# Two pairs of stages merged into one interleaved program, and norms on GpSimd cut in halves

## The chip, the cores and the metric

One core of one Trainium2 chip runs the whole kernel. The metric is the device time of that core in microseconds, as the median of three runs. TensorE is called PE, VectorE DVE, ScalarE ACT, GpSimd POOL, and SP is the engine that issues most transfers.

## The reference

Four batches (B) of 512 tokens with 128 features pass through two layers. Cut to what matters here:

```python
x = L0_attn_x                                           # first layer
x = x + 0.5 * L0_ffn(layernorm(x))                      # latent causal attention, mixture of 8 experts
x = x + L0_attn(layernorm(x))                           # full attention, 16 heads
x = x + 0.5 * L0_ffn(layernorm(x))
x = x + 0.5 * L1_ffn(layernorm(x))                      # second layer: heads of chosen tokens
x = x + L1_attn(layernorm(x))                           # four depths of additive attention and MLP
x = x + 0.5 * L1_ffn(layernorm(x))                      # heads of chosen tokens again
```

`L1_ffn` lets each of 8 heads choose 64 of the 512 tokens by a gate, and attends among these:

```python
logits = sigmoid(einsum('bth,eh->bte', X, Wr))
topk_vals, topk_I = top_k(logits.transpose(0, 2, 1), k)            # k = 64
Q, K, V = split(einsum('beki,eij->bekj', Xg, Wqkv), 3)             # Xg: the chosen tokens
Q, K = rope(Q, topk_I), rope(K, topk_I)
A = softmax(where(topk_I[..., :, None] >= topk_I[..., None, :], Q @ K.T / sqrt(HP), -inf))
out = out.at[idx_flat].add((A @ V * topk_vals[..., None]) @ Wo)
```

A depth of `L1_attn` is, for i in 0 to 3:

```python
h = layernorm(x); q = l2norm(h @ Wq[i] + bq[i]); k = l2norm(h @ Wk[i] + bk[i])
A = l2norm(q @ w_g[i] * SCALE, axis=tokens); G = sum(A * q, axis=tokens)
x = x + ((G * k) @ Wp[i] + bp[i] + q) @ Wf[i] + bf[i]
x = x + gelu(layernorm(x) @ W1[i] + b1[i]) @ W2[i] + b2[i]
```

## The kernel before

`X` and `Y` stay in SBUF as 128 partitions by batch, 4 chunks of tokens and 128 features. All work is written as Python generators that yield between steps. The order in which they are advanced is the order in which instructions are written; each engine then runs a queue of its own, and the queue's order is fixed when the program is built, where an instruction that is ready can be placed ahead of one written earlier. Tiles come from pools. A pool with `bufs=2` has two buffers of each tile, and a pool that is opened after another is closed gets the same memory, so that its first writers wait for the last users.

**First layer.** `first_layer` makes twelve tasks, four batches each of latent, full and latent attention, of 10, 16 and 10 units. `attention()` walks over the units, two half steps to a unit: PE computes scores (L527 for the row maxima, L562 shifted for the exponent), ACT the exponent (L574), POOL the causal masks (L580), PE the products (L605). After each half step `step_background` advances the first generator of `background` and all of `beside`. `prepare` of the next task stands in `background`: layer norm, with `h` (L323) and for latent tasks `Y` (L336) made by POOL in four pieces of 128x128 each, then the transposes and projections. `place` waits for `prepare` and for the end of the task before last, plus `GAP`, then spreads q and k over the partitions. `gates` stands in `beside`: norm (four pieces on POOL, L686), gate logits, expert weights. `Mixture` computes the experts (L472, L473 on POOL) in the half steps that follow.

**Second layer, three stages.** `choice` takes two batches: layer norm into `m_yg` (L182, with the rows of `m_trig` loaded beside), logits (L809), sigmoid with Abs and Exp on ACT (L815, L816), eight rounds of max and replace on DVE (L836, L838), a scan (L846), and the slot numbers `byt` (L854). `chosen_attention` runs the heads of a batch: `pick` (L869, DVE) gathers tokens by matmuls (L880), then projections (L903), rotation (`other`, L917 and L918 on DVE, an add on POOL at L921), scores (L931, L932), Exp (L939), products (L961, L970), and the way back into `X` (L983, L992). Its 15 steps start five apart for neighbouring batches, and the choice of batches 2 and 3 (`others`) starts with it. `additive_attention` runs the four depths of the four batches, with a start five steps apart, 23 steps to a depth: L1142 and L1145, the norms `r` on POOL (L154), L1176, L1188, L1199, L1205, L1209, then the MLP with L1244, Gelu on ACT (L1245), L1250 and L1259. `weights(i)` loads one depth's weights on SP (L1035 to L1045) and folds them by matmuls (L1058 to L1104). Weights 0 are made before the first step, weights i from step 23 (i - 1) + 15 on. At the end a choice of batches 0 and 1 runs beside the last depth.

`in_turn` advances a list of generators, each once in a round. The loop at the end of `tile_macaron` runs `first_layer` and `chosen_attention`, then `additive_attention` and `chosen_attention`, each with pools of its own: `moa` for the heads, `add` and `one` for the depths, `top` for the choices.

Of the kernel before, what the change touches and what calls it, by code (L numbers as in the profile page):

```python
# [8 lines left out]
F32 = mybir.dt.float32  # L9
BF16 = mybir.dt.bfloat16  # L10
AF = mybir.ActivationFunctionType
ALU = mybir.AluOpType
# [28 lines left out]
def tile_macaron(ctx: ExitStack, tc: tile.TileContext, a: dict, out: bass.AP):  # L41
# [31 lines left out]

    def load(name, shape, src, eng=nc.scalar):
        t = const.tile(shape, F32, name=f"sb_{name}")
        eng.dma_start(t, src)
        return t
# [16 lines left out]
    causal = const.tile([P, T], F32, name="causal")  # L94
    paired = const.tile([P, P], BF16, name="paired")
    ones = const.tile([P, T], F32, name="ones")
    zeros = const.tile([4, T], F32, name="zeros")
    before = const.tile([P, NE, NE], F32, name="before")
# [103 lines left out]
    def later(name, shape, *parts):  # L202


        def begin():
            if name not in late:
                late[name] = const.tile(shape, F32, name=f"sb_{name}")
            for where, src in parts:
                dst = late[name] if where is None else late[name][:, where]
                tc.keep_in_program_order(nc.sync.dma_start(dst, src))  # L210

        return begin
# [19 lines left out]
    def first_layer(opened, picked):  # L232
        with (
# [42 lines left out]
            class Task:  # L276
# [24 lines left out]
                def prepare(self):  # L301
# [19 lines left out]
                    for c in range(NC):  # L321
                        at = n - NC + c
                        eng.tensor_scalar(  # L323
                            h[:, c, :], X[:, b, c, :], mv[:, c, 0:1], r[:, at : at + 1], ALU.subtract, ALU.mult
                        )
                    yield
# [7 lines left out]
                    else:  # L334
# [4 lines left out]
                        nc.scalar.activation(hT, transposed(h), AF.Copy, scale=f_cols[:, 0:1])  # L339
                        yield  # L340
# [332 lines left out]
            def gates(task):  # L673
# [11 lines left out]
                for c in range(NC):  # L685
                    nc.gpsimd.tensor_scalar(h[:, c, :], Y[:, b, c, :], r[:, c : c + 1], None, ALU.mult)  # L686
                yield
# [170 lines left out]
    def chosen_attention(top, picked, choosing):  # L858

        with tc.tile_pool(name="moa", bufs=2) as wp:  # L860

            def stream(b):

                yg, byt = picked[b]

                pick = wp.tile([P, NC, NE, KSEL], F32, name="pick")
                for c in range(NC):
                    at = byt[:, c, :].unsqueeze(2).to_broadcast([P, NE, KSEL])
                    nc.vector.tensor_tensor(  # L869
                        pick[:, c], at, slots.unsqueeze(1).to_broadcast([P, NE, KSEL]), ALU.is_equal  # L870
                    )
                yield

                xs = wp.tile([P, NPAIR, YG], F32, name="xs")
                for k in range(2):
                    ps = bank().rearrange("p (i n) -> p i n", i=2)
                    for i in range(2):
                        r = 2 * k + i
                        for c in range(NC):
                            nc.tensor.matmul(  # L880
                                ps[:, i, 0:YG],
                                lhsT=pick[:, c, 2 * r : 2 * r + 2, :].rearrange("p e s -> p (e s)"),
                                rhs=yg[:, c, :],
                                start=(c == 0),
                                stop=(c == NC - 1),
                            )
                    (nc.scalar.copy if k else nc.vector.tensor_copy)(xs[:, 2 * k : 2 * k + 2, :], ps[:, :, 0:YG])
                    yield
                xg = wp.tile([P, T], F32, name="xg")
                nc.scalar.copy(xg, transposed(xs[:, :, 0:P]))  # L890
                own = small.tile([P, NPAIR, NE], F32, name="own")
                nc.gpsimd.tensor_tensor(own, xs[:, :, AT_G : AT_G + NE], mine, op=ALU.mult)
                gate = small.tile([P, NPAIR], F32, name="gate")
                nc.vector.tensor_reduce(gate, own, axis=AX.X, op=ALU.add)
                yield

                qk = wp.tile([P, NPAIR, 2, P], F32, name="qk")
                v = wp.tile([P, NPAIR, P], F32, name="v")
                for r in range(NPAIR):
                    ps = bank()  # L900
                    for i in range(2):
                        e = 2 * r + i
                        nc.tensor.matmul(  # L903
                            ps[i * KSEL : (i + 1) * KSEL, 0 : 3 * P],
                            lhsT=xg[:, e * KSEL : (e + 1) * KSEL],
                            rhs=late["m_wqkv"][:, e, :],
                            start=True,
                            stop=True,
                        )
                    both = ps[:, 0 : 2 * P].rearrange("p (k n) -> p k n", k=2)  # L910
                    halves = both[:, :, 0:NROT].rearrange("p k (h n) -> p k h n", h=2)
                    cos = xs[:, r, P : P + HROT].unsqueeze(1).unsqueeze(1).to_broadcast([P, 2, 2, HROT])
                    sin = xs[:, r, P + HROT : P + NROT].unsqueeze(1).to_broadcast([P, 2, HROT])
                    turned = qk[:, r, :, 0:NROT].rearrange("p k (h n) -> p k h n", h=2)
                    nc.vector.tensor_tensor(turned, halves, cos, ALU.mult)
                    other = wp.tile([P, 2, 2, HROT], F32, name="other")
                    nc.vector.scalar_tensor_tensor(other[:, :, 0, :], halves[:, :, 1, :], -1.0, sin, ALU.mult, ALU.mult)  # L917
                    nc.vector.tensor_tensor(other[:, :, 1, :], halves[:, :, 0, :], sin, ALU.mult)  # L918
                    nc.scalar.copy(qk[:, r, :, NROT:P], both[:, :, NROT:P])
                    nc.scalar.copy(v[:, r, :], ps[:, 2 * P : 3 * P])  # L920
                    nc.gpsimd.tensor_tensor(turned, turned, other, op=ALU.add)  # L921
                    yield
                qT = wp.tile([P, T], F32, name="qT")
                nc.scalar.copy(qT, transposed(qk[:, :, 0, :]))
                kT = wp.tile([P, T], F32, name="kT")
                nc.vector.tensor_copy(kT, transposed(qk[:, :, 1, :]))
                yield
                pscore = bank()
                for r in range(NPAIR):
                    cols = slice(r * P, (r + 1) * P)  # L930
                    nc.tensor.matmul(pscore[:, cols], lhsT=qT[:, cols], rhs=kT[:, cols], start=True, stop=False)  # L931
                    nc.tensor.matmul(pscore[:, cols], lhsT=ident_h, rhs=paired, start=False, stop=True)  # L932
                nm = small.tile([P, NPAIR], F32, name="nmp")
                nc.vector.tensor_reduce(nm, by_chunk(pscore), axis=AX.X, op=ALU.max, negate=True)
                nc.vector.tensor_scalar(nm, nm, P**-0.5, None, ALU.mult)
                total = small.tile([P, NPAIR], F32, name="totalp")
                e_ = wp.tile([P, NPAIR, P], F32, name="e_")
                for r in range(NPAIR):
                    nc.scalar.activation(  # L939
                        e_[:, r, :],  # L940
                        pscore[:, r * P : (r + 1) * P],
                        AF.Exp,
                        bias=nm[:, r : r + 1],
                        scale=P**-0.5,
                        accum_out=total[:, r : r + 1],
                    )
                rt = small.tile([P, NPAIR], F32, name="rtp")
                nc.vector.reciprocal(rt, total)

                back = wp.tile([P, NPAIR, T], F32, name="back")  # L950
                for r in range(NPAIR):
                    nc.vector.tensor_scalar(
                        back[:, r, :], places, xs[:, r, AT_T : AT_T + 1], gate[:, r : r + 1], ALU.is_equal, ALU.mult
                    )
                yield
                eT = wp.tile([P, NPAIR, P], F32, name="eT")
                nc.vector.tensor_copy(eT, by_chunk(transposed(e_)))
                yield
                pav = bank()
                for r in range(NPAIR):  # L960
                    nc.tensor.matmul(  # L961
                        pav[:, r * P : (r + 1) * P], lhsT=v[:, r, :], rhs=eT[:, r, :], start=True, stop=True
                    )
                av = wp.tile([P, T], F32, name="av")
                nc.scalar.copy(av, pav)
                yield
# [397 lines left out]
```

## Time and profile before

| | |
|---|---|
| runs | 1371.43, 1371.81, 1377.16 us; median 1371.81 |
| profiled execution | 1375.36 us, of which 1373.6 us from the first to the last instruction |
| mean granted PE clock | 0.968 |
| PE idle while waiting (by line waited for) | heads' and depths' norms: `h` L1225 8.7 us, `m_yg` L182 6.8 us; masks `e` L580 7.5 us |
| POOL `r` (L154) | 64 of 128x4, mean 1125 ns; 16 of 128x8, mean 1648 ns |
| DVE max and replace (L836, L838) | 32 each, about 0.67 us |
| SP | 4 sets of six weight loads for the depths, 256, 128, 256, 129, 256 and 256 KB |

The page is read from the engine that is busiest down to the places where it isn't: the span is cut in 40 equal slices, and each digit gives a busy share or a clock in tenths. Windows give the same for chosen stretches, in us with the number of instructions in brackets, in the order PE, PE weight loads, DVE, ACT, POOL, then clock, DMA share and GB/s. In timelines and groups, the bracket at the end says how long the engine sat idle before and which instruction released it. A matmul in fp32 leaves two records.

### The profile page before, as it was taken

Reading aid. Unit: us, or ns where it says so; the run is one execution under the profiler, and the core shown is the slowest. Engines: PE = TensorE matmul, PEld = TensorE weight load, DVE = VectorE, ACT = ScalarE, POOL = GpSimd, SP = SyncE. Lnnn points to the kernel's source line nnn. Section 1 sums busy time; section 2 is a strip of 40 time slices with the busy share of each in tenths; the row PEclk is TensorE's granted clock in tenths of the full one; section 3 lists DMA queues with packets and bytes.
Section 4 is the critical chain, followed back from the end, with each engine's and each line's share of the span. In section 5 each row is a group of like instructions: output and inputs, shape, how many; then the busy total and the mean of one; then the engine's idle time right before and its main releaser. Section 6 shows DMA issues by size and latency. Waiting matters only on the chain.

```text
span 1373.6 us, 29346 instructions
## 1 busy us (share of the span) xinstructions
PE 1288.2 (94%) x11050; PEld 699.2 (51%) x11050; DVE 953.5 (69%) x3293; ACT 587.1 (43%) x1180; POOL 563.3 (41%) x823
## 2 busy tenths in 40 slices
PE   5998999999999999999999999989799999997897
PEld 2554444333333333465444443466667767665675
DVE  6886676666657777878767548687466776667773
ACT  1555454454546666655545443222123332323122
POOL 8345655544424202025564655622144443543100
PEclk8999999999999999999999999999969999999799
DMA  3001111020111100000101021000300000000000
GB/s 115 21 24 43 40 33 49 2 80 1 64 44 32 38 2 18 18 3 19 60 22 46 20 71 40 32 0 17 100 20 5 16 1 16 1 1 1 1 9 23
DMA packets 37172, 39.52 MB, mean 29 GB/s; under 512 B 11080, under 2 KB 23880, under 8 KB 37032
## 3 DMA queue, kind: packets, MB, share of 16 engines
q1 hardware_dynamic: 34536, 35.06, 8.1%
q10 hardware_dynamic: 2496, 2.59, 0.6%
q8 instruction: 87, 1.43, 0.4%
q14 instruction: 53, 0.43, 0.1%
HBM read 29.45 MB, written 1.18 MB: 22 GB/s over the span
## 4 chain that ended last, share of the span: by engine, by line
PE 71%; DVE 17%; POOL 9%; issue 2%; ACT 1%; DMA 0%; SPq 0%; DVEq 0%; POOLq 0%; ACTq 0%
PE bank L562 17%; PE sum L605 10%; PE bank L267 10%; PE sum L267 7%; PE bank L527 6%; POOL r L154 4%; PE bank L193 4%; PE bank L880 2%; PE bank L983 2%; DVE st L167 2%; PE bank L1250 2%; PE bank L903 1%; PE bank L1142 1%; PE bank L1244 1%; DVE junk L543 1%
## 5 line engine op out<-in xcount | busy, mean ns | idle before, releaser
L574 ACT ACTIVATE e<-bank 128x512 f32<-128x512 f32 x576 | 313.9, 595 | 276.5 <-PE bank L527 238.0
L527 PE MATMUL bank<-kA,qA 32*128 32x512 f32 (+3 forms) x1536 | 345.6, 524 | 3.8 <-DVE nm L543 1.8
L562 PE MATMUL bank<-qA,kA 32*128 32x512 f32 (+3 forms) x1536 | 331.9, 521 | 0.3 <-DVE nm L543 0.3
L543 DVE CUSTOM_DVE_ANT_0 junk<-bank,causal 128x384 f32<-128x384 f32 (+3 forms) x512 | 251.0, 490 | 88.4 <-PE bank L527 50.2
L547 DVE TENSOR_REDUCE nm<-bank 128x1 f32<-128x512 f32 x256 | 164.9, 686 | 77.4 <-PE bank L527 77.0
L473 POOL TENSOR_TENSOR hid<-v,spread 128x512 f32<-128x512 f32 x128 | 164.1, 1288 | 126.0 <-DVE v L472 101.5
L562 PEld LDWEIGHTS bank<-qA,kA 32*128 32x128 f32 x1536 | 128.5, 184 | 136.6 <-issue 54.8
L605 PE MATMUL sum<-e,vA 128*32 128x256 f32 (+1 forms) x2560 | 183.1, 367 | 7.5 <-POOL e L580 7.5
L580 POOL TENSOR_SCALAR_AFFINE_SELECT e<-e 128x256 f32<-128x256 f32 x256 | 99.7, 409 | 191.3 <-ACT e L574 190.3
L527 PEld LDWEIGHTS bank<-kA,qA 32*128 32x128 f32 x1536 | 146.0, 185 | 23.8 <-DVE nm L543 5.8
L605 PEld LDWEIGHTS sum<-e,vA 128*32 128x32 f32 x2560 | 62.7, 109 | 166.5 <-issue 133.6
L267 PE MATMUL sum<-hid,sb_f_w 128*32 128x512 f32 x1024 | 135.6, 597 | 2.8 <-POOL hid L473 2.7
L267 PE MATMUL bank<-tT,sb_f_w 128*32 128x512 f32 x1024 | 137.1, 602 | 0.0
L472 DVE SCALAR_TENSOR_TENSOR v<-th,bank 128x512 f32<-128x512 f32 x128 | 87.1, 681 | 43.3 <-ACT th L467 28.4
L467 ACT ACTIVATE th<-bank 128x512 f32<-128x512 f32 x128 | 76.4, 598 | 48.5 <-PE bank L267 39.0
L154 POOL TENSOR_TENSOR r<-v,mhalf 128x4 f32<-128x4 f32 (+1 forms) x64 | 71.9, 1125 | 5.1
L1244 PE MATMUL bank<-h2T,w 128*128 128x512 f32 x128 | 69.0, 632 | 0.2 <-ACT h2T L1233 0.2
L1250 PE MATMUL bank<-w,hid 128*128 128x128 f32 x512 | 65.6, 277 | 0.1
L1250 PEld LDWEIGHTS bank<-w,hid 128*128 128x128 f32 x512 | 62.9, 194 | 4.8 <-issue 1.5
L1245 ACT ACTIVATE hid<-bank,sb_l_cols 128x512 f32<-128x512 f32 x64 | 44.0, 689 | 40.1 <-PE bank L1244 39.8
L1142 PE MATMUL bank<-wa,hT 128*128 128x385 f32 x128 | 57.6, 547 | 2.5 <-ACT hT L1135 2.5
L312 POOL TENSOR_SCALAR v<-mv 128x4 f32<-128x4 f32 x12 | 2.8, 231 | 130.8 <-DVE mv L171 130.5
(279 smaller groups left out, 1807.9 us busy)
## 6 DMA issues: line engine op xcount, KB each, us to landing
spread<-away SPq DMA_DIRECT2D x64, 256.0 KB
qA<-mT SPq DMA_DIRECT2D x192, 2.0 KB
qA<-qC SPq DMA_DIRECT2D x11, 256.0 KB
kA<-kC SPq DMA_DIRECT2D x11, 256.0 KB
w<-in_l_w_dram SPq DMA_DIRECT2D x8, 256.0 KB
sb_m_wqkv<-in_m_wqkv_dram SPq DMA_DIRECT2D x4, 384.0 KB
m_yg<-in_m_trig_dram SPq DMA_DIRECT2D x8, 130.0 KB
X<-in_x_dram SPq DMA_DIRECT2D x4, 256.0 KB
```

The source lines that it names most:

```text
L154: last_root[0] = nc.gpsimd.tensor_tensor(r[:, 0:n], src, mhalf[:, 0:n], op=ALU.pow).ins
L267: nc.tensor.matmul(ps[32 * j : 32 * j + 32, :], lhsT=w[:, 32 * j : 32 * j + 32], rhs=rhs, start=start, stop=stop, skip_group_check=True,)
L472: nc.vector.scalar_tensor_tensor(v, th, 1.0, ph, ALU.add, ALU.mult)
L473: nc.gpsimd.tensor_tensor(hid, v, self.spread[e], op=ALU.mult)
L527: nc.tensor.matmul(ps[:, at : at + w], lhsT=t.qA[r0 : r0 + 32, g, c * P : (c + 1) * P], rhs=t.kA[r0 : r0 + 32, g, 0:w], start=True, stop=True,
L543: nc.vector.tensor_tensor_reduce(junk[:, 0:w], src, causal[:, T - w : T], 1.0, NEG, ALU.add, ALU.max, dst)
L547: nc.vector.tensor_reduce(dst, src, axis=AX.X, op=ALU.max)
L562: nc.tensor.matmul(ps[:, at : at + w], lhsT=t.kA[r0 : r0 + 32, g, kc * P : (kc + 1) * P], rhs=t.qA[r0 : r0 + 32, g, q0:T], start=True, sto ...
L574: nc.scalar.activation(es[n][:, j, :], ps, AF.Exp)
L580: nc.gpsimd.affine_select(out=e, in_=e, pattern=[[0, 2], [1, P]], compare_op=ALU.is_ge, fill=0.0, base=0, channel_multiplier=-1,)
L605: nc.tensor.matmul(to[32 * j : 32 * j + 32, q0 + lo - at : q0 + hi - at], lhsT=t.vA[:, kc, 4 * j + g, :], rhs=es[n][:, j, lo:hi], start=fresh,
L1250: nc.tensor.matmul(pm[:, c * P : (c + 1) * P], lhsT=hid[:, f, c * P : (c + 1) * P], rhs=w2[:, f, :], start=(f == 0), stop=(f == 3),)
```

## The change

The two stages of the heads and the stage of the depths become `heads_of_chosen` and `additive_attention`, which return generators, and `second_layer` runs them all in one `in_turn`, in one set of pools. The bodies are the same but for the lines shown. A batch's depths begin when its heads are done and the batch before it is five steps ahead. Weights i begin when batch 0 is 13 steps into depth i - 1 and the last batch has finished depth i - 2. The choice of batches 2 and 3 begins when the heads of batch 1 have begun. Some tiles get one buffer in place of two, since all pools now stand side by side. Tiles that only the first layer uses move to a pool `firsts`, which is closed after it. In the first layer, `prepare` and `gates` yield in the middle of the four pieces of their norms on POOL.

```diff
+    until_first = ExitStack()
+    firsts = until_first.enter_context(tc.tile_pool(name="firsts", bufs=1))
...
@@ prepare
                         eng.tensor_scalar(
                             h[:, c, :], X[:, b, c, :], mv[:, c, 0:1], r[:, at : at + 1], ALU.subtract, ALU.mult
                         )
+                        if c == 1 and self.k:
+                            yield
                     yield
...
                             nc.gpsimd.tensor_scalar(
                                 Y[:, b, c, :], X[:, b, c, :], mv[:, c, 0:1], r[:, c : c + 1], ALU.subtract, ALU.mult
                             )
-                        nc.scalar.activation(hT, transposed(h), AF.Copy, scale=f_cols[:, 0:1])
-                        yield
+                            if c == 1:
+                                nc.scalar.activation(hT, transposed(h), AF.Copy, scale=f_cols[:, 0:1])
+                                yield
@@ gates
                     nc.gpsimd.tensor_scalar(h[:, c, :], Y[:, b, c, :], r[:, c : c + 1], None, ALU.mult)
+                    if c == 1:
+                        yield
                 yield
@@ heads_of_chosen
-                pick = wp.tile([P, NC, NE, KSEL], F32, name="pick")
+            pick = wp.tile([P, NC, NE, KSEL], F32, name="pick", bufs=1)
...
+            qk = wp.tile([P, NPAIR, 2, P], F32, name="qk", bufs=1)
...
+                other = wp.tile([P, 2, 2, HROT], F32, name="other", bufs=1)
...
+            qT = wp.tile([P, T], F32, name="qT", bufs=1)
+            kT = wp.tile([P, T], F32, name="kT", bufs=1)
+            eT = wp.tile([P, NPAIR, P], F32, name="eT", bufs=1)
+            av = wp.tile([P, T], F32, name="av", bufs=1)
@@ additive_attention, weights: wqk, bqk, wpT, wfg, L and bpw with bufs=1
-                for _ in range(3):
+            for _ in range(3 if i else 6):
                     yield
@@ additive_attention, stream
             for i in range(DEPTH):
+                while i not in ready:
+                    yield
...
+    def second_layer(top, picked, choosing):
+        STEPS = 23
+        with (
+            tc.tile_pool(name="moa", bufs=2) as cp,
+            tc.tile_pool(name="add", bufs=2) as wp,
+            tc.tile_pool(name="one", bufs=1) as hp,
+        ):
+            heads = heads_of_chosen(cp)
+            additive, weights, depths = additive_attention(wp, hp)
+            again = {}
+            done = {picked_: [0] * B for picked_ in (0, 1)}
+            deep, through = [0] * B, set()
+            def headed(n, b):
+                now = (picked, again)[n]
+                while b not in now or (b > 0 and done[n][b - 1] < 5):
+                    yield
+                for _ in heads(b, now):
+                    done[n][b] += 1
+                    yield
+                done[n][b] = 99
+            def deepened(b):
+                while done[0][b] < 99 or (b > 0 and deep[b - 1] < STEPS // B):
+                    yield
+                for _ in additive(b):
+                    deep[b] += 1
+                    yield
+                deep[b] += STEPS
+                through.add(b)
+            def prepared(i):
+                while i > 0 and (deep[0] < STEPS * (i - 1) + 13 or depths[B - 1] < i - 1):
+                    yield
+                yield from weights(i)
+            def chosen(now, n):
+                while done[n][1] < 1:
+                    yield
+                yield from choice([2, 3], (lambda b: True) if n == 0 else through.__contains__, top, now)
+            def chosen_again():
+                while min(done[0]) < 99:
+                    yield
+                yield from choice([0, 1], through.__contains__, top, again)
+            in_turn(
+                [(0, choosing)]
+                + [(0, headed(0, b)) for b in range(B)]
+                + [(0, chosen(picked, 0))]
+                + [(0, deepened(b)) for b in range(B)]
+                + [(0, prepared(i)) for i in range(DEPTH)]
+                + [(0, chosen_again())]
+                + [(0, headed(1, b)) for b in range(B)]
+                + [(0, chosen(again, 1))]
             )
...
+        chosen_first = first_layer(opened, {})
+        until_first.close()
+        second_layer(*chosen_first)
```

## Prediction

> **What bounds the kernel now.** I read the page first (busy shares, slices, chain), then the waits of PE, then tables of windows, then timelines at the places where the windows show holes.
>
> ```profile
> PE 1288.2 (94%) x11050; PEld 699.2 (51%) x11050; DVE 953.5 (69%) x3293; ACT 587.1 (43%) x1180; POOL 563.3 (41%) x823
> ...
> PE   5998999999999999999999999989799999997897
> ...
> PEclk8999999999999999999999999999969999999799
> ...
> PE 71%; DVE 17%; POOL 9%; issue 2%; ACT 1%; DMA 0%; SPq 0%; DVEq 0%; POOLq 0%; ACTq 0%
> ```
>
> The reader is to see an engine that works nearly always: 1373.6 - 1288.2 = 85.4 us of the span have no matmul. So the change can give only where PE has holes or a slow clock. Slices 29 (busy) and 30 (clock) and slices 37 and 38 (both) say where, at 34.3 us each: 962 to 1030 us and 1236 to 1305 us. Windows there (columns: engine busy us and count, then the clock):
>
> ```profile
> 990.00:1000.00 10.00, 6.42 (x26) 4.07 (x26) 6.39 (x45) 1.93 (x7) 3.20 (x3) 0.81 0.05 14
> ...
> 1260.00:1270.00 10.00, 5.52 (x44) 4.86 (x44) 9.13 (x22) 1.32 (x3) 1.62 (x3) 0.96 0.01 2
> 1270.00:1280.00 10.00, 4.32 (x16) 3.01 (x16) 7.67 (x23) 1.12 (x3) 1.27 (x2) 0.50 0.00 0
> ```
>
> The first hole is a wall between stages, as the timeline shows:
>
> ```profile
> 974.30 3.84 PE L983 MATMUL bank<-xp,back 128*128 128x128 f32 x32 [0.80 <-DVE xp L978]
> ...
> 978.37 0.29 POOL L1017 TENSOR_SCALAR_AFFINE_SELECT fold<-ident 128x128 f32<-128x128 f32 x1 [6.52 <-PE bank L983]
> ...
> 983.97 1.13 PE L1058 MATMUL bank<-wfg,wpT 128*128 128x128 f32 x8 [1.34 <-DMA wfg<-in_l_wfg_dram]
> ```
>
> `fold` needs only `ident`, yet it waits for the last matmul of the heads: its memory was theirs. Weights load behind that wall too. The second layer therefore runs as: first heads 885.2 (first `pick` 885.8) to 978.3; depths to 1267.1 (last L1260); a choice on DVE until the next `pick` at 1280.3; second heads to 1370.1: 484.9 us.
>
> **The change, part by part.** I count in ticks (one round of `in_turn`), by following the yields. A tick is an order, not a wall: an L (L1049) due in tick 41 of the depths runs at 982.67. In the new program, with tick 0 at the first `pick`: heads 0 and 1 run from 0 to 15 and 4 to 19, the choice of batches 2 and 3 from 4 to 16 (now from 0), heads 2 and 3 from 17 to 32 and 21 to 36. Depths start at 15, 19, 32, 36. Weights 2 wait until batch 3 has done its first depth (59) and are ready at 66; batches 0 and 1 wait 5 ticks and 1 tick for them and run in step from there to 113; batches 2 and 3 end at 124 and 128. The second choice of 0 and 1 takes 113 to 125, then the heads.
>
> Rates: one depth of four batches takes 66.4 us, the distance of these two lines in the chain of waits:
>
> ```profile
> 1100.99 1.65 POOL r L154
> ...
> 1167.37 1.64 POOL r L154
> ```
>
> It has 92 batch-ticks and one set of weights. The weights' matmuls, 34 records at about 0.112 us (L1250 x16 takes 1.79), are 3.9 us, 4.3 at PE's share below. So a batch-tick costs (66.4 - 4.3)/92 = 0.675 us. PE's own work in a batch-depth is, from chain pieces, L1244 3.4, L1250 3.6, L1142 2.8, L1205 0.9, L1176 0.9, rest 2.2 = 13.8; 4 x 13.8 + 3.9 = 59.1 of 66.4, so 89%. A head: L880 5.9, L983 3.85, L903 2.9, transposes 2, scores 1.2, L961 1.1, L970 1.1 = 18.0 us, 20.2 at 89%.
>
> - Ticks 0 to 15: DVE sets it. A head: pick 4 x 0.68, back 4 x 0.55, five groups of 0.68, turns 4 x 0.70, rest 1.2 = 12.3; a choice: eight rounds of 1.41, norms 6.8, rest 5.2 = 23.3; a weight set 3.2. Head 0, three quarters of head 1, choice and weights: 12.3 + 9.2 + 23.3 + 3.2 = 48 us.
> - 15 to 38: heads 2 and 3 (40.4), the end of head 1 (6.7), weights 1 (4.3) and 23 + 19 + 6 + 2 = 50 batch-ticks (33.8): 85.2. DVE has about 54 in it.
> - 38 to 61: 92 batch-ticks, 62.1. 61 to 113: 200 batch-ticks and two weight sets, 135 + 8.6 = 143.6.
> - 113 to 125: the chain of a choice, measured 36.8 (last X of batch 1 at 1243.4 to `byt` at 1280.2); the last 26 batch-ticks (16 us of PE) lie under it, where now only about 15 do.
> - From 125: the second heads as measured, 89.8.
>
> Sum 48 + 85.2 + 62.1 + 143.6 + 36.8 + 89.8 = 465.5, against 484.9: **19.4 us less**. Of it 8 at the first joint: batch 0 ends its first depth at 1034.4, 149.2 us after the start, with 62 batch-ticks done by all; the sum has 133.2 for 50 and 8.1 for 12 more, 141.3. The other 11 are at the last.
>
> What is late next: at the first joint DVE's choice, at the last the same choice, which still has a serial 12 us of rounds.
>
> The pool `firsts` gives its memory back before the second layer and adds no instruction. The moved weights count with their DMAs. Six issues (1.28 MB) stand on SP from tick 0 and landed within 10 us at 978 to 988; the first use is at tick 6, and heads cover them. Behind them on SP come the `m_trig` rows of the choice, needed 13 ticks later. Without cover the 1.3 + 0.5 us of PE's present waits would return. POOL gets `fold` and the memsets (0.5 us) earlier, ahead of `own`; free.
>
> **One buffer instead of two.** `pick` of head 1 must wait for L880 of head 0 (5.9 us), where seven picks ran back to back at 1280.4; the 2.7 us of DVE then lie beside head 0's L903 (2.9); behind it on DVE wait the choice's norms. `other` puts a POOL add (0.54) between two turns, some 0.45 us in three of four. Nothing like it is in the trace: between 0 and 11 us (8 heads x 3 x 0.45), nearest to L903's cadence of 0.72 per r, which hides most: 3. Behind a waiting `other` on DVE stand the choice's rounds. Single weights, `qk`, `qT`, `eT`, `av` come back 5 or more ticks later: nothing. Weight loads that wait on SP for them have only the next choice's `m_trig` behind them.
>
> **Tables, where a rule speaks against the change.** Exp (heads, choice) and Gelu (depths) now share a program.
>
> ```profile
> 1257.20 1.28 ACT L816 ACT_TABLE_LOAD   x1
> 1258.50 0.26 ACT L816 ACTIVATE ez<-ez 128x64 f32<-128x64 f32 x1
> ```
>
> The Trainium skill, "ScalarE: Activation LUTs", What ACT_TABLE_LOAD costs, gives 2.66 us a switch, load and drain, and wants functions of a set grouped. The row has 1.28 and the next function 1.30 after the start: no drain that shows. By ticks head 3's Exp (30) precedes the first Gelu (32), so 0 to 4 switches are added: 0 to 5 us of ACT by the row, 0 to 11 by the rule. ACT is 35% busy; 1 us by the row (forecast 2 later by the rule).
>
> **First layer.** POOL's norms block the masks:
>
> ```profile
> 103.30 3.15 POOL L323 TENSOR_SCALAR h<-X,mv,r 128x128 f32<-128x128 f32 x4
> 106.43 3.28 POOL L336 TENSOR_SCALAR Y<-X,mv,r 128x128 f32<-128x128 f32 x4
> 109.67 1.50 POOL L580 TENSOR_SCALAR_AFFINE_SELECT e<-e 128x256 f32<-128x256 f32 x4
> ```
>
> PE lost 3.8 us there to `e`, and 2.3 and 1.4 near 650; with the holes around (3.3 + 0.8, then 2.3 + 2.3) and a clock of 0.73 after the first, 11 us in all. In twos a mask waits 1.6, not 6.4. Gain 0 (a mask already slips between pieces at 648.71) to 11; I take 5. The added half step (about 2.9 us) of `prepare` is covered: 7 of the 12 that `place` leaves; that of `gates` by the mixture before it. If not, one half step, 3 us.
>
> **Sum:** 19.4 + 5 - 3 - 1 = 20.4. The profiled run is 1375.4 (span 1373.6 and 1.8 around it): 1355.0. The median of the runs, 1371.8, is 0.26% lower: **1351**; its own range 1339 to 1360.
>
> **The clock, rule against row.** Idle of PE between 960 and 1020 is 10.9 us; from 997.5 to 1020 the clock is 0.50 while PE shows 20.2 of 22.5 busy. "TensorE: Matmul & The Clock Gate", Part 1, releases the clock after some 3.4 us of activity: 1.7 us lost. By the row half of 20.2, 10.1, is lost. All bubbles of this joint are thus 21 by the row, 12.6 by the rule; my sum takes 8 of them, since DVE's first 48 us stay.
>
> **Rivals.**
> 1. The mixed streams close the holes fully: 12 more at the first joint (4 by the clock rule) and 9 at the last: idle of PE there is 1.5 + 2.7 (1230 to 1250) and 4.5 + 5.7 (1260 to 1280), half of 11.3 busy at the slow clock (1267.5 to 1287.5) 5.6, together 20, of which my sum has 11. 1351 - 21 = 1330. For it: independent work on every engine. Against: the choice's serial DVE.
> 2. DVE and its order take the first joint back, as at 910 to 920 where DVE is 9.95 of 10 busy and PE 6.68, and the halved norms give nothing: 20.4 - 8 - 5 = 7.4 gained, 1364. Against: DVE 54 of 85 us.
> 3. Slower: waiting for weights 2 puts batches 0 and 1 in step, and from tick 61 to 113 their chains (seven POOL and DVE handovers a depth) coincide. Price per tick: 2.76 in the sum; below it cannot go by PE. At 3.4 the 52 ticks cost 33 more: 1384. It decides from 2.76 + 20.4/52 = 3.15. Against: batches 2 and 3 are 12 and 16 ticks off and fill with Gelu and L1250 just then.
> 4. That the walls stay (memory reused all the same) is in rival 2: the depths' pools open with the heads', so they share no memory.
>
> **Numbers.** Forecast 48%, rival 1 24%, rival 2 16%, rival 3 12%. Range 1326 to 1371: rival 1's middle and rival 2 in, most of rival 3 out. Half a per cent (6.9 us) is what a measurement tells: faster 0.48 + 0.24 + half of rival 2 = 0.80; same 0.09; slower 0.11.
>
> **What would show it.** `fold` and weights near 890; depths' L1142 under the second pair of heads, PE at 9 or more of 10 from 930 to 1020 and no clock of 0.5 there; no `pick` later than about 1265; at most 8 table loads; PE's wait for `e` under 4 us. Wrong: ticks 61 to 113 over 164 us, or PE below 8.5 of 10 in the mixed part.

## The result and the profile after

The changed kernel takes **1406.6 us** (median of 4 runs, 1404.4 to 1410.0), the kernel before, run beside it, 1373.3 (1371.4 to 1377.2): a ratio of 1.0244, 95% interval 1.0215 to 1.0272. It is slower by 33 us where 20 less were forecast.

The page of the changed kernel: busy sums, slices of PE and of its clock, shares of the chain that ended last.

```profile
PE 1300.3 (93%) x11050; PEld 711.3 (51%) x11050; DVE 966.0 (69%) x3293; ACT 584.3 (42%) x1180; POOL 562.8 (40%) x823
...
PE   6998999999999999998999998979989998987888
...
PEclk8999999999999999999999999998998999897899
...
PE 73%; DVE 16%; POOL 7%; issue 2%; ACT 1%; DMA 1%; DVEq 0%; ACTq 0%; POOLq 0%; SPq 0%
```

The same 11050 matmuls take 12 us more of PE time (1288.2 before). A slice is 34 to 35 us. The single clock of 6 of the kernel before (slice 30) is gone, but a clock of 8 or 7 now stands in five of the last thirteen slices (28, 31, 35, 37, 38) where the kernel before had two low ones (30 and 38), and PE's dips are spread in the same way. A table of windows cuts the second layer at the forecast's ticks 0, 38, 61 and 113 and at the second heads (columns: window, us, then busy us and count of PE, PEld, DVE, ACT and POOL, the granted clock, DMA share, GB/s):

```profile
892.00:1026.00 134.00, 120.23 (x769) 94.37 (x770) 99.00 (x377) 34.12 (x108) 36.37 (x53) 0.94 0.11 31
1026.00:1093.00 67.00, 61.56 (x320) 46.12 (x319) 45.83 (x239) 19.73 (x40) 29.30 (x33) 0.87 0.03 9
1093.00:1251.00 158.00, 144.61 (x789) 107.08 (x788) 99.09 (x530) 44.84 (x95) 61.88 (x68) 0.91 0.03 9
1251.00:1303.00 52.00, 33.35 (x169) 25.80 (x167) 37.41 (x138) 10.95 (x16) 17.99 (x22) 0.76 0.00 0
1303.00:1400.00 97.00, 85.52 (x560) 67.10 (x560) 59.64 (x153) 23.32 (x84) 9.48 (x22) 0.95 0.03 9
```

Exact edges, by the starts of the lines: first `pick` 892.0; the ends of a depth (L1253) at 1025.9 (batch 0, first), 1093.3 (batch 0, second) and 1252.5 (batch 1, fourth); `pick` again at 1302.6; end of the heads 1399.5.

| stage | forecast, us | changed, us |
|---|---|---|
| ticks 0 to 38 | 133.2 | 133.9 |
| 38 to 61 | 62.1 | 67.4 |
| 61 to 113 | 143.6 | 159.2 |
| choice of 0 and 1 | 36.8 | 50.1 |
| second heads | 89.8 | 96.9 |
| sum | 465.5 | 507.5 |

The first stage is as forecast; everything after it is too long. And the first `pick` comes at 892.0, not 5 us ahead of the 885.8 of before but 6 behind.

### The profile page after: what moved, and what is told of

It is laid out like the page before. It is cut to its first block, busy times and chain, and to the rows that moved or that the text cites. A ratio compares the mean times of both kernels' runs of the same rounds, so it can differ in the third digit from the quotient of the medians.

```text
span 1402.6 us, 29382 instructions
## 1 busy us (share of the span) xinstructions
PE 1300.3 (93%) x11050; PEld 711.3 (51%) x11050; DVE 966.0 (69%) x3293; ACT 584.3 (42%) x1180; POOL 562.8 (40%) x823
## 4 chain that ended last, share of the span: by engine, by line
PE 73%; DVE 16%; POOL 7%; issue 2%; ACT 1%; DMA 1%; DVEq 0%; ACTq 0%; POOLq 0%; SPq 0%
PE bank L568 17%; PE sum L611 10%; PE bank L270 9%; PE sum L270 7%; PE bank L533 6%; PE bank L196 4%; POOL r L157 4%; PE bank L885 3%; PE bank L1244 2%; PE bank L1136 2%; PE bank L908 2%; PE bank L1238 2%; DVE st L170 2%; DVE junk L549 1%; PE bank L988 1%
## 5 line engine op out<-in xcount | busy, mean ns | idle before, releaser
L885 PE MATMUL bank<-m_yg,pick 128*128 128x201 f32 x256 | 55.4, 375 | 6.7 <-DVE pick L874 6.7
```

Of the source, the lines that this page charges most:

```text
L885: nc.tensor.matmul(ps[:, i, 0:YG], lhsT=pick[:, c, 2 * r : 2 * r + 2, :].rearrange("p e s -> p (e s)"), rhs=yg[:, c, :], start=(c == 0), s ...
```

## The experiments

Another cut serves for comparing the runs: first `pick`; batch 3's first depth ends; its last depth ends; the last head ends. (In the runs that kept the old stages, depths 1 to 4 of batch 3 are the same work.) Runs of the kernel before beside the five groups had medians of 1373.3 to 1376.6.

| run | median, us | ratio, 95% | first `pick` | to batch 3's first depth | to its last | to the end |
|---|---|---|---|---|---|---|
| before | 1371.8 | | 885.8 | 192.4 | 186.9 | 105.0 |
| changed | 1406.6 | 1.0215 to 1.0272 | 892.0 | 196.2 | 205.1 | 106.2 |
| e1_norms | 1385.0 | 1.0056 to 1.0128 | 892.0 | 192.6 | 185.6 | 105.3 |
| e2_layer | 1398.6 | 1.0156 to 1.0206 | 887.4 | 195.2 | 204.8 | 106.2 |
| e3_in_step | 1407.8 | 1.0221 to 1.0270 | 888.2 | 205.5 | 207.0 | 101.6 |
| e4_choice_early | 1409.0 | 1.0213 to 1.0276 | 896.1 | 198.1 | 205.1 | 105.0 |
| e6_hold | 1406.8 | 1.0205 to 1.0252 | 894.5 | 196.2 | 198.6 | 112.6 |
| e7_late | 1381.6 | 1.0025 to 1.0062 | 893.7 | 185.7 | 185.1 | 111.4 |
| e8_prepare | 1382.2 | 1.0024 to 1.0058 | 891.2 | 194.3 | 186.7 | 104.8 |
| e9_gates | 1382.9 | 1.0038 to 1.0074 | 891.0 | 193.7 | 185.8 | 104.6 |
| e10_late_choice | 1362.6 | 0.9888 to 0.9953 | 887.8 | 180.2 | 185.0 | 103.7 |
| e11_choice_now | 1371.9 | 0.9951 to 0.9981 | 896.5 | 182.2 | 185.1 | 103.2 |
| e14_first_now | 1375.1 | 0.9960 to 1.0003 | 894.5 | 175.2 | 185.2 | 107.5 |
| e15_last_now | 1404.2 | 1.0185 to 1.0233 | 894.1 | 192.1 | 205.2 | 105.0 |
| e16_whole_now | 1365.0 | 0.9871 to 0.9936 | 887.9 | 179.1 | 188.1 | 107.2 |

The columns say at once where the changed kernel loses: 18 us in three depths of batch 3, 6 ahead of the second layer, 4 at the first joint. Three causes were thought of at the outset: batches in step share their stalls, the choice of batches 2 and 3 is late, the halved norms cost.

**The two parts of the change, alone.** e1_norms is the kernel before with the halved steps of `prepare` and `gates` (the three places of the change) and nothing else.

> The kernel before with only the first layer's norms cut in halves. Theory: the halves are behind the 6 us by which the first layer ended later (first pick at 891.9 instead of 885.8), since half a step more lies before each mask's products: 4 to 8 us slower, near 1379. Rival, as the prediction had it: masks wait less, 0 to 11 us faster, near 1367. Third: the later end comes from the second layer's weights and memory, then no change, within 2 us.

e2_layer is the changed kernel with those lines taken back.

> The changed kernel with the first layer's norms in one piece of four again, so the second layer alone is changed. Theory: 23 to 27 of the 29 us are the second layer's, so 1396 to 1400. If the first layer's end depends on what follows it (weights and choice placed among its last steps) the time stays near 1404.

Measured 1385.0 and 1398.6: 9.7 and 23.4 us over the kernel before that ran beside them, which make up the 33. Both parts cost; the larger is the second layer.

**In step, in the old stages.** e3_in_step has nothing of the change; its batches start in the depths at steps 0, 0, 12 and 15 in place of 0, 5, 10 and 15.

```diff
-            runs = [(STEPS // B * b, stream(b)) for b in range(B)]
+            runs = [((0, 0, 12, 15)[b], stream(b)) for b in range(B)]
```

> The kernel before with its four batches started in the depths at steps 0, 0, 12 and 15 in place of 0, 5, 10, 15: the first two in step, as the changed kernel has them after waiting for weights 2, and nothing else changed. Theory (being in step costs PE its cover and its clock): the period of a depth grows from 66.4 to 70 us or more, 10 to 20 us slower in all, near 1385. Rival (the loss is the wait itself, or the choices at the end): the period stays within 1 us of 66.4 and the time within 4 us of before.

1407.8: the spacing alone costs 32 us, as much as the change. The windows from the end of batch 3's first depth to that of its last, of the kernel before, of e3_in_step and of the changed kernel (columns as above):

```profile
1078.20:1265.10 186.90, 174.15 (x1015) 129.41 (x1014) 127.32 (x668) 61.90 (x117) 81.96 (x93) 0.97 0.01 4
```

```profile
1093.70:1300.70 207.00, 189.72 (x992) 144.60 (x992) 126.41 (x656) 60.29 (x117) 78.01 (x87) 0.87 0.01 3
```

```profile
1088.20:1293.30 205.10, 182.18 (x984) 136.44 (x983) 130.84 (x659) 56.48 (x112) 78.39 (x88) 0.89 0.03 9
```

With no more matmuls in the window PE is busy 8 to 16 us longer, because the clock is 0.87 and 0.89 and not 0.97; and it is idle 4.5 to 10 us longer. The reading is that two batches in step want the same engine together and wait for the same engine together; the windows show what it costs, not that.

**Which delay puts them in step?** Three runs came first; two of them missed what was expected. e4_choice_early lets the last choice begin as soon as the one before is done:

```diff
-                while done[n][1] < 1:
+                while (done[n][1] < 1) if n == 0 else (0 not in now):
                     yield
```

> The changed kernel, where the last choice of batches 2 and 3 begins as soon as the choice of 0 and 1 is done, as in the kernel before, in place of waiting for the heads of batch 1 to begin. Theory (the order at the end costs the 7 us by which the second heads take longer, 96.9 against 89.8): 5 to 8 us faster than the changed kernel, near 1399. Rival (the choice waits for something else, as DVE's queue): within 2 us of 1406.

1409.0, no effect. e6_hold parts batches 0 and 1 again after the wait for the third weights:

```diff
                 while i not in ready:
                     yield
+                for _ in range(5 if (b, i) == (1, 2) else 0):
+                    yield
```

> The changed kernel, with batch 1 held for five steps behind batch 0 after the wait for the third weights, so that the two are not in step in the second depth. Theory (being in step costs the second half): as the kernel before with starts 0, 0, 12, 15 lost 32 us over four depths, ticks 61 to 113 fall from 158 to about 146, batch 3's depths end 8 to 14 us earlier, and the whole takes about 1395 us. Rival (the loss comes from the work of choices and heads beside the depths, not from the spacing): within 3 us of the changed kernel, about 1405.

The depths gave 6.5 us (205.1 to 198.6), less than the 8 to 14 expected, and the tail took 6.4 back (106.2 to 112.6): batch 1 now ends later, so the choice of 0 and 1 starts later. Nothing was gained on the whole. e7_late gives up the early start of the depths:

```diff
-                while done[0][b] < 99 or (b > 0 and deep[b - 1] < STEPS // B):
+                while done[0][b] < 99 or (b == 0 and done[0][B - 1] < 1) or (b > 0 and deep[b - 1] < STEPS // B):
                     yield
```

> The changed kernel, with batch 0's depths held until the heads of batch 3 begin, so that the four batches keep distances of about five ticks and the third weights are ready without a wait; the last batch ends its depths at the same tick (128) as in the changed kernel. Theory (spacing decides, and the early start of batches 0 and 1 buys nothing, because the last batch's end sets the time): the four depths run at about 66 us each as in the kernel before, batch 3 ends its depths near 1277 instead of 1295, and the whole takes about 1383 us (1378 to 1388). Rival (the early start was worth what it took, so giving it up costs as much as the spacing brings): about 1405.

1381.6, as expected: 25 us come back, and starting two batches sooner is worth nothing while the last one ends at the same tick. By the ticks batch 0 is due for the third weights at 67 and they are ready at 66, so nobody waits for them.

These two runs also show what is not settled. When the third depths end, the batches stand nearly equally far apart in both: 15.7, 18.1 and 14.9 us in e6_hold, 14.0, 17.9 and 14.6 in e7_late (1.8, 36.6 and 16.2 in the changed kernel). From the end of batch 2's second depth to that of batch 0's last lie 35 ticks, with 140 batch-ticks and one weight set in each of these runs. They take, in the changed kernel, e6_hold, e7_late and e14_first_now (which comes next):

```profile
1139.70:1249.70 110.00, 100.04 (x538) 73.08 (x538) 67.17 (x349) 31.23 (x64) 41.46 (x46) 0.91 0.02 6
```

```profile
1141.60:1250.00 108.40, 97.51 (x527) 71.70 (x527) 68.90 (x369) 30.35 (x62) 43.32 (x48) 0.92 0.02 6
```

```profile
1130.80:1228.50 97.70, 90.21 (x527) 64.75 (x526) 65.65 (x364) 30.48 (x62) 43.36 (x48) 1.00 0.02 6
```

```profile
1122.40:1219.40 97.00, 89.84 (x522) 66.95 (x522) 65.85 (x354) 30.28 (x62) 41.95 (x47) 0.98 0.02 6
```

So parting batches 0 and 1 after they have stood still for the third weights is not enough: e6_hold stays at the slow price. Being in step costs (e3_in_step shows it in the old stages), but in the changed kernel it is not shown to be all of the loss; why e6_hold stays slow was not separated.

**The wait in `chosen`.** In e7_late `pick` of batch 2 still came 57 us after that of batch 0 (43 before). e11_choice_now removes the wait in `chosen` from both choices of batches 2 and 3 of the changed kernel; e10_late_choice does so in the second layer of e2_layer with the hold of e7_late; e14_first_now and e15_last_now remove it from one of the two choices each; e16_whole_now is e11_choice_now with whole norms.

```diff
             def chosen(now, n):
-                while done[n][1] < 1:
-                    yield
                 yield from choice([2, 3], ...)
```

e14_first_now and then e15_last_now:

```diff
-                while done[n][1] < 1:
+                while n == 1 and done[n][1] < 1:
```

```diff
-                while done[n][1] < 1:
+                while (done[0][1] < 1) if n == 0 else 2 not in through:
```

> The second layer as one program in turn with whole norms, batch 0's depths held until the heads of batch 3 begin (that alone gave 1381.6 us with halved norms), and the choice of batches 2 and 3 taken up at once instead of waiting for the first step of batch 1's heads. Theory (the tail is the chain choice of 0 and 1, choice of 2 and 3, heads of 2 and 3, and the wait for batch 1's heads put 13 us into it: picks of batch 2 came 52 us after those of batch 0, against 39 in the kernel before): the tail from batch 3's last depth falls from 111 to about 100 us, whole norms give 6 to 8 us, together 1360 to 1366 us, under the kernel before. Rival (the engines are full there, so an earlier choice only slows the heads of 0 and 1): about 1375 us, no better than the kernel before.

> The changed kernel, halved norms and all, with only the wait for batch 1's heads taken from both choices of batches 2 and 3. Theory (the wait delays the chain that ends last by about 9 us at the end, and 10 us or more at the first joint, where picks of batch 2 came 57 us after those of batch 0 against 43 before): about 1392 us, and the picks of batch 2 come some 45 us after those of batch 0. Rival (starting the last choice with the end of the one before changed nothing, so this won't either): about 1406 us.

> The changed kernel with the wait for batch 1's heads taken from the first choice of batches 2 and 3 alone; the last one keeps it. Theory (the first wait holds batches 2 and 3 back, so that the third weights come late and batches 0 and 1 fall in step: with both waits gone 14 of the 35 us came before the first depth of batch 3 ended, 22 in the depths and 2 in the tail): nearly all of it, 1372 to 1380 us, batch 3's depths ending some 185 us after its first. Rival (the last wait is on the chain that ends last): 1395 us or more.

> The changed kernel with the wait taken from the last choice of batches 2 and 3 alone (it starts when batch 2's depths are through). Theory: the tail from batch 3's last depth loses 2 to 8 us and nothing else moves, 1398 to 1405 us. Rival (the last wait is what costs): 1372 to 1385 us.

> The changed kernel with whole norms in the first layer and without either wait. Theory (the parts add: 1371.9 with halved norms, which cost 7 to 10 us): 1362 to 1366 us, level with the version that also holds batch 0's depths (1362.6), so that the hold is worth nothing once the third weights come in time. Rival (the hold still buys even distances between the batches): 1367 us or more.

e11_choice_now takes 1371.9: the two lines are worth **35 us**, far more than the 14 expected. e14_first_now has 1375.1 and e15_last_now 1404.2, so it is the *first* wait, worth 31.5 alone; the last, on the chain that ends last, gives 2, within the scatter of the runs. e10_late_choice (1362.6) and e16_whole_now (1365.0) are level: with the third weights in time the hold buys nothing that shows. Both are faster than the kernel before, by 0.8 and 1.0%, and than the changed one.

How the wait works is seen on DVE's timeline (start, us, engine, line). The changed kernel:

```profile
892.04 2.50 DVE L874 TENSOR_TENSOR pick<-byt,slots 128x512 f32<-128x512 f32 x4
...
914.88 0.69 DVE L811 COPY yT<-bank 128x512 f32<-128x512 f32 x1
...
948.32 0.23 DVE L862 COPY byt<-bank 128x64 f32<-128x64 f32 x1 [0.15 <-PE bank L860]
```

and e14_first_now:

```profile
892.94 0.69 DVE L811 COPY yT<-bank 128x512 f32<-128x512 f32 x1 [3.09 <-PE bank L196]
...
894.54 2.50 DVE L874 TENSOR_TENSOR pick<-byt,slots 128x512 f32<-128x512 f32 x4
...
937.88 0.23 DVE L862 COPY byt<-bank 128x64 f32<-128x64 f32 x1 [1.30 <-PE bank L860]
```

The transposed norm `yT` of batches 2 and 3 comes 23 us after the first `pick` in the one and 2 us ahead of it in the other; `byt`, which their heads need, 56 and 43 us after. In ticks: without the wait batch 3 ends its first depth at 55, not 59, the third weights are ready at 62 and not 66, and batches 0 and 1, due at 61 and 65, begin their third depth at 63 and 65 and not both at 67. The last piece of the third weights (`crow`) and the norms that begin the third depths (`hs`, four to a batch), in the changed kernel and in e14_first_now:

```profile
1110.01 0.28 DVE L1098 TENSOR_TENSOR crow<-bank,sb_l_rows 128x128 f32<-128x128 f32 x1
...
1113.77 2.56 DVE L1118 TENSOR_SCALAR hs<-Y,mv,r 128x127 f32<-128x127 f32 x6
```

```profile
1093.68 0.29 DVE L1098 TENSOR_TENSOR crow<-bank,sb_l_rows 128x128 f32<-128x128 f32 x1
...
1097.08 0.60 DVE L1118 TENSOR_SCALAR hs<-Y,mv,r 128x127 f32<-128x127 f32 x2
...
1104.88 1.29 DVE L1118 TENSOR_SCALAR hs<-Y,mv,r 128x127 f32<-128x127 f32 x1
```

In the changed kernel six of the eight norms stand in one row, those of two batches; in e14_first_now the second batch follows 7.8 us later. The third depths of batches 0 and 1 end, in the changed kernel and in e14_first_now:

```profile
1177.34 0.69 DVE L1253 TENSOR_TENSOR Y<-bank,Y 128x512 f32<-128x512 f32 x1 [1.23 <-PE bank L1244]
1179.13 0.69 DVE L1253 TENSOR_TENSOR Y<-bank,Y 128x512 f32<-128x512 f32 x1
```

```profile
1156.08 0.69 DVE L1253 TENSOR_TENSOR Y<-bank,Y 128x512 f32<-128x512 f32 x1 [1.23 <-PE bank L1244]
1164.96 0.68 DVE L1253 TENSOR_TENSOR Y<-bank,Y 128x512 f32<-128x512 f32 x1
```

1.8 us apart against 8.9. Not all of the gain is in the depths, though: against the changed kernel e14_first_now saves 21.0 us up to the end of batch 3's first depth, where the heads of batches 2 and 3 start 13 us sooner, and 19.9 in the three depths after it, while its first `pick` is 2.5 us later and its tail 1.3 longer. The window of batch 3's depths in e14_first_now stands against the three above:

```profile
1069.70:1254.90 185.20, 171.85 (x1004) 128.51 (x1003) 129.39 (x668) 59.75 (x118) 80.25 (x92) 0.97 0.03 10
```

**Which halved norm costs?** e8_prepare has the first two hunks of e1_norms alone, e9_gates the last alone.

> The kernel before, with the halved background steps in the norms of `prepare` alone (h and Y there), `gates` left whole. The two together took 1385.0 against 1375.3. Theory A (the longer norm queues ahead of the masks through `prepare`, which has two norms of four pieces, one of them beside the first chunk's masks): most of the 9.7 us, so about 1382 us. Theory B (it is `gates`, whose step stands beside the spread of the experts): about 1376 us.

> The kernel before, with the halved background step in the norm of `gates` alone. Theory A (`prepare` costs): about 1377 us. Theory B (`gates` costs): about 1382 us. If the two parts add up, this one and the one with `prepare` alone have excesses that sum to about 9.7 us; if they don't, the place of the steps in the background's round is what matters and not the length of a step.

6.7 and 7.4 us: each costs, so neither theory holds. By the first `pick` they do not add: 5.4 and 5.2 us later than before, and 6.2 with both. The whole times cannot tell, since 6.7 + 7.4 lies inside the interval of e1_norms (1.0056 to 1.0128, 8 to 18 us). For `gates` the place can be seen: TensorE at the end of the first layer, in the kernel before and in e9_gates.

```profile
863.60 0.42 PE L852 MATMUL bank<-ident,slot 16*128 16x16 f32 x4
863.95 1.40 PE L267 MATMUL sum<-hid,sb_f_w 128*32 128x512 f32 x8
```

```profile
861.64 0.42 PE L854 MATMUL bank<-ident,slot 16*128 16x16 f32 x4 [1.17 <-DVE slot L850]
865.61 8.12 PE L267 MATMUL sum<-hid,sb_f_w 128*32 128x512 f32 x48 [3.56 <-DVE byt L856]
```

Both kernels reach the slot transposes with the experts' products still to do. With the half step more, those products come, by the releasers that the trace infers, after the choice's `slot` and `byt`: 1.2 and 3.6 us idle, and the clock is at half from 864 to 871. The changed kernel has the same wait (3.6 us for `byt`) and the same cold stretch, 865 to 872. In e8_prepare it is another place (a half clock from 651 to 668); why the halved norm of `prepare` leads there was not separated. The first `pick` sorts the runs: with halved norms in both places 892.0 to 896.5 (eight kernels), with whole norms 885.8 to 888.3.

**Is the half clock cause or sign?** Four small products that nobody reads stand ahead of four matmul groups in each depth: e13_warm is the kernel before with them, e12_warm_step is e3_in_step with them.

```diff
+    def warm(ps):
+        for _ in range(4):
+            nc.tensor.matmul(ps[:, P : 2 * P], lhsT=ident_h, rhs=paired, start=True, stop=True)
...
                     pn = bank()
+                    warm(pn)
```

(and likewise ahead of the products with `wg` and of the transposes of both norms)

> The kernel before with depth starts 0, 0, 12, 15 (1407.75 us) and four small bf16 products that nobody reads put ahead of four matmul groups of each depth at which TensorE waits (the transposes of both norms, the products with the weights w and with wg). By the trace of the run without them, 22.5 of the 32 us lost were matmuls at half clock and 9.7 idle time. Theory (short idle spells let the clock fall, and work that fills them keeps it up): the half-clock time after 850 us falls from 113 us to under 80, and the whole to about 1395 us, the products' own time (64 groups of some 0.25 us, partly in idle time) taken off. Rival (the clock falls for another reason, or the fill is too little): half-clock time as before, and 5 to 15 us slower, 1413 to 1422.

> The kernel before with the same small products at the same places, as the price of the fill where the clock is hardly down in the depths (one half-clock stretch of 7 us there). Theory: nothing to win but that stretch, so 5 to 15 us slower, 1380 to 1390 us; if the fill were free, 1373.

1385.7 for e13_warm (ratio 1.0042 to 1.0099) and 1409.7 for e12_warm_step (1.0201 to 1.0280). The fill costs about 9 us where the clock is up and 2 in step, so some 7 come back there; the intervals of the two runs are as wide as that, so the times alone do not show it. Summed over the trace after 850 us, the half clock of e3_in_step falls from 112.7 to 92.4 us and PE's work inside it from 96.6 to 80.9; half of that, 7.9, fits. So by the trace the clock is in part a cause, but the expected fall under 80 and the 1395 us were missed, and the fill pays for itself nowhere.

## Why the prediction was wrong, by its own steps

- **What bounds it: right.** PE, its holes and its clock decide; every gain and loss above is in those two.
- **Ticks 0 to 38: right in size** (133.9 for 133.2), but the gain of 8 us at this joint is batch 0's. Batch 3, on which the end hangs, ended its first depth 3.8 us later than before (196.2 against 192.4). The sum looked at who starts sooner, not at who ends last.
- **The step that failed: "61 to 113: 200 batch-ticks and two weight sets, 135 + 8.6 = 143.6"**, measured 159.2, with 38 to 61 5.3 us over as well. A price per batch-tick, taken from batches five ticks apart, was used where the text itself had counted batches 0 and 1 in step. It had counted the cause too, "the choice of batches 2 and 3 from 4 to 16 (now from 0)", and gave those four ticks no price. The 35 ticks shown above cost 98.8 us at its price (140 x 0.675 + 4.3) and took 110.0, which is 0.755 for a batch-tick; in e14_first_now they took 97.0. With that wait gone (e14_first_now) the same five terms measure 128.4 + 62.0 + 140.7 + 40.9 + 95.9 = 467.9, in e11_choice_now 135.4 + 62.0 + 140.6 + 40.8 + 91.7 = 470.5, against the forecast's 465.5: the sum described the kernel without the wait. How far it is the being in step and how far the standing still for weights that raises the price stays open, because e6_hold, parted but late, took 108.4. (The profiled run of e14_first_now is 8 us under the median of its runs, that of e11_choice_now at it.)
- **Choice of 0 and 1, and second heads:** 13.3 and 7.1 us over. The first is mostly the same cause: without the first wait it takes 40.9. The second is not, and its cause is open: 95.9 stays with the last wait, and without it the second heads take 91.7, 95.7 and 95.7 us (e11_choice_now, e15_last_now, e16_whole_now).
- **First layer: wrong in sign.** Forecast 5 us gained; measured 6 later. The mask waits, which were to shrink under 4 us, grew from 7.5 to 9.7 in three waits, as the waits of PE show:

```profile
PE sum L611 <- POOL e L586: 9.7, 3, 4.4
```

  and the half step of `gates`, costed at nothing "by the mixture before it. If not, one half step, 3 us", was not covered: a wait of 3.6 us and the slow clock behind it. Nor was that of `prepare`, by the 6.7 us of e8_prepare.
- **Tables:** the second layer has as many loads as before, four, so nothing is lost, by the row's 1.28 us or by the 2.66 of the Trainium skill, "ScalarE: Activation LUTs", whose rule to batch calls by set stands under "Table sets: the hidden batching unit". ACT was 28% busy in the second layer before, 135.1 of 485.0 us, and not 35%. The loads in the changed kernel (line, operation, count, busy us, mean ns):

```profile
L1239 ACT ACT_TABLE_LOAD x2 | 2.6, 1283 | 0.0
L824 ACT ACT_TABLE_LOAD x2 | 2.6, 1283 | 0.0
```

- **One buffer, 3 us:** not tried alone. The wait is there, `pick` of the second head starts 8.0 and 9.2 us after the first head's (3.4 and 2.4 before), but its price isn't known. The sum holds within 2.4 to 5 us without it in two runs, so it is not large in these.
- **Rivals:** the third, at 12%, comes nearest to what happened. Its price per tick was above what was measured, 159.2/52 = 3.06 and not 3.4; its point of decision, 3.15, was not reached, and the kernel is slower all the same, because it charged the spacing to those 52 ticks alone, and the losses of the other four stages (26 us) and the later first `pick` (6) were in no case. So the signs for "wrong" (over 164 us, PE under 8.5 of 10) did not show either: 159.2 us, and PE 120.23 of 134 in the mixed part.
- **Other signs:** `fold` was made at 819.4, earlier than forecast; weights and depths mixed with the heads as said; but half clock stood at 943.5 to 953.8 in the mixed part, and the `pick` of the second heads came at 1302.6, not by 1265.

The ledger against the profiled execution: 42.0 us over the sum of the second layer, 11.2 in the first layer (6.2 later for 5 sooner), less the 4 set aside for buffers and tables, make 49.2; forecast 1355.0 and measured 1404.4 differ by 49.4.

## What to carry to other kernels

When streams are interleaved by hand, price the distance between them as well as their work: a rate measured with streams well apart and never waiting did not hold here once a common wait held them up and lined them up. Before starting some of them sooner, follow the one that ends last, and ask which shared step (here the third weights, which wait for the slowest batch) makes the early ones wait for it. Here a wait of four ticks, far from the end, cost 31.5 us, and one on the last chain 2.

## What the runs showed of the hardware

The clock fell on less than was expected. In e3_in_step, the windows around one stretch (columns as above):

```profile
1138.10:1145.00 6.90, 5.99 (x36) 4.04 (x34) 3.47 (x19) 3.14 (x6) 4.79 (x4) 1.00 0.00 0
1145.00:1155.30 10.30, 10.30 (x39) 8.62 (x40) 3.33 (x17) 0.69 (x1) 1.06 (x2) 0.50 0.00 0
1155.30:1165.00 9.70, 8.14 (x64) 7.13 (x62) 7.27 (x40) 1.96 (x3) 4.33 (x7) 1.00 0.18 53
```

After 0.9 us of idle in 6.9, TensorE is at half clock for 10.3 us with no gap in its work as the trace has it. Before the steady stretches of this run the idle time in the 7 us ahead was 0.9 to 2.3 us, and the stretches lasted 6.8, 10.2 or 20.5 us, multiples of 3.4. The Trainium skill, "TensorE: Matmul & The Clock Gate", Part 1, puts the fall after an idle window of some 3.4 us and the return after as long a busy one; here shorter lulls sufficed and the return took up to three such windows of unbroken work. What counts as busy for the clock no run here shows; products of a single column (L1176 and L1188) fill about 3.5 us of that stretch. So 0.9 us of idle took some 5 more with it there (half of 10.3), and kernels with equal work differ in busy time as well as in idle time: after 850 us e3_in_step has 22.5 us more PE time than the kernel before and 9.7 more of idle, the changed kernel 12.9 and 16.1.

The best of the runs, e10_late_choice, shows the opposite, in its page's slices:

```profile
PE   5998999999999999999899999998989999987887
...
PEclk8997999999999999999999999998999999999799
```

Between 946.6 and 1257.3 us, the whole of the depths, no stretch is at half clock (10.2 us are in the mixed joint ahead of it), and its half clock after 850 us adds up to 29.9 us, against 69.0 in the kernel before and 106.2 in the changed one.
